# Cross attention of a decoder layer: outputs turned and divided in 32x32 blocks on VectorE instead of with TensorE transposes

## The chip, the cores and the metric

One core of a Trainium2 chip runs the whole program. The metric is device time in microseconds (us), and shares are of the profiled execution's span. Everything is float32.

## What is computed

The program is one layer of a decoder over 32 sequences of 128 tokens by 512 features: self attention, cross attention, and a mixture of experts. Each of the three adds its result to x. The change lies in cross attention, which reads each sequence as 128 channels by 512 positions:

```python
def _L0_xattn_ref(x, c, Wq, bq, Wk, bk, Wv, bv, Wo, bo):   # x, c: (32, 128, 512)
    ...
    q = split_heads(_proj(x, Wq, bq))      # 8 heads of 16 channels
    k = split_heads(_proj(c, Wk, bk))
    v = split_heads(_proj(c, Wv, bv))
    q = _apply_rotary(q_emb, q)
    k = _apply_rotary(k_emb, k)
    scores = jnp.einsum('bhtc,bhsc->bhts', q, k) / math.sqrt(K_CH)
    p_attn = jax.nn.softmax(scores, axis=-1)
    out = jnp.einsum('bhts,bhsc->bhtc', p_attn, v)
    out = out.transpose(0, 1, 3, 2).reshape(b, N_HEADS * K_CH, t_t)
    return _proj(out, Wo, bo)
...
x = x + _L0_xattn_ref(_layernorm(x), ctx_2048, ...)
```

## The kernel before, in words

**Stages.** Self attention runs first, then cross attention (from about 942 us to about 2145 us of the span), then the experts. Routing of the tokens to the experts (class Routing) is done in small steps inside the cross-attention stage.

**Cross attention.** For each sequence b, the eight heads are held as four pairs of 32 rows; one head of each pair is "side" 0, the other is side 1. A unit of work is a step (b, side, c, pair): 2 sides, 4 chunks c of 128 positions and 2 pairs of row groups make 16 steps for a sequence and 512 in all. In step n

- `maxima` multiplies q and k (L615, two matmuls of 32 rows x 128 columns by 512) and VectorE takes the negated row maxima straight from PSUM (L619, 128x1024);
- `exponentials` multiplies k and q again for the step 11 earlier (L638), and ScalarE takes exponentials from PSUM (L642, 128x1024).

The maxima of a side are turned with TensorE (`turn_maxima`, L83 on nm) and added into q (L627), so that the second product comes out with its maximum taken off. When all eight steps of a side are through, `weigh` multiplies the exponentials with the values (L653, 32 matmuls of 32 columns in two halves). The values carry a block of ones beside each head's 16 channels, so that of the 32 rows of a row group 16 are the head's outputs and the others its sum. The result is one PSUM tile of 128 rows by 512 positions per side, and still has to be divided by the sums.

**Division before the change.** ScalarE copies each side's result to SBUF (`xu`, L659). `divide` turns both sides with eight 128x128 TensorE transposes (L668) into one PSUM tile, so that positions lie on partitions and the sums in columns; VectorE takes their reciprocal (L671) and multiplies (L674, once for each side, from PSUM) into `xo`. `turn_out` turns `xo` back with four transposes (L83 on xo) and ScalarE copies that to `xoT` (L682). `leave` multiplies with the output weights (L691), and VectorE adds bias and residue (L695).

**What sets the order.** The order on TensorE, VectorE, ScalarE and GpSimd in this stage is the order of the calls (`tc.manual_schedule`). `plan` gives each piece of work of sequence b a step, counted from the sequence's own first step (16 b); `advance` then runs step n as: first half of `weigh` if one is due, the "sooner" calls, `maxima`, `exponentials`, second half of `weigh`, the "later" calls. Counted modulo 16, so that "step 13" is the step with remainder 13, the work falls as follows (each entry is for some earlier or later sequence):

| step | before maxima | maxima, exponentials | after |
|---|---|---|---|
| 13 | weigh side 1, first half; slots_of, measure_out, rotate q | yes | weigh side 1, second half, then copy to xu; groups |
| 14 | | yes | values |
| 15 | | yes | divide; normalize_out; enter |
| 0 | | yes | turn_out |
| 1 | | yes | turn_maxima side 1; enter |
| 2 | | yes | leave |
| 3, 4 | | yes | at 4: project k; enter |
| 5 | weigh side 0, first half; choose, rotate k, measure | yes | weigh side 0, second half, then copy to xu; take |
| 6 | | yes | hand_over (L83 on h); enter |
| 7, 8 | | yes | count (L934), then router (L718) |
| 9 to 12 | | yes | turn_maxima side 0, project q, enter |

Those VectorE operations of these calls that matter below: `groups` is five small ones (L878, L879, L881, L885, L887), `take` two (L922 with two SBUF inputs, L927).

**PSUM.** All tiles of PSUM come from one pool of four buffers of two banks each (`banks()`, L50). A new tile takes the buffer whose last reader stands earliest in the order of the calls. In the built program the matmuls of `exponentials` (L638) therefore wait in most steps for VectorE, and those of `maxima` (L615) in most steps for ScalarE.

Of the kernel before, what the change touches and what calls it, by code (L numbers as in the profile page):

```python
# [10 lines left out]
F32 = mybir.dt.float32  # L11
I32 = mybir.dt.int32
AF = mybir.ActivationFunctionType
ALU = mybir.AluOpType
# [4 lines left out]
P = 128  # L19
E = 512  # L20
# [82 lines left out]
def self_attention(cm, x, x1_d, Wq, Wk, Wv, Wo, lq1, lk1, lq2, lk2, heads, beside):  # L103
# [13 lines left out]
    with ExitStack() as ctx:  # L117
# [301 lines left out]
        for n in range(len(steps) + 5):  # L419
# [11 lines left out]
            if 2 in at:  # L431
                weigh(*at[2])
            if k % 2:
                values(g + 1, k // 2)
            elif 5 in at:
                leave(at[5][0])
            if 3 in at and at[3][1]:
                scale_out(at[3][0])
            if 2 in at:
                divide(*at[2])  # L440
                if at[2][1]:
                    finish(at[2][0])
            b = (g + 2) * G + k // 2
            if k % 2 == 0:
                measure(b)
                if 4 in at:
                    load_again(at[4][0])
            else:
                normalize(b)
                turn_in(b)  # L450
                load(b + G)
                if 4 in at:
                    turn_out(at[4][0])
# [4 lines left out]
class CrossAttention:  # L458
# [10 lines left out]

    NH, C = 8, 16
    TC = EC
    S = 2 * TC
    Q = P // 32
# [169 lines left out]
    def weigh(self, b, side, half):  # L645

        TC, Q, po = self.TC, self.Q, self.po
        if half == 0:
            po[b, side] = self.cm.banks()[:, 0, :]
        for c in (2 * half, 2 * half + 1):  # L650
            es = [self.expd.pop((b, side, c, pair)) for pair in range(2)]
            for j in range(Q):
                self.nc.tensor.matmul(  # L653
                    po[b, side][ts(j, 32), :], self.v2[b % 2][:, c, 2 * j + side, :],
                    es[j // 2][:, j % 2, :], start=c == 0, stop=c == TC - 1,
                )
        if half:
            self.out[b, side] = self.p2.tile([P, E], F32, name="xu")
            self.nc.scalar.copy(self.out[b, side], po.pop((b, side)))  # L659

    def divide(self, b):

        nc, TC, Q, C, out = self.nc, self.TC, self.Q, self.C, self.out
        tr = self.cm.banks()
        for side in range(2):
            u = out.pop((b, side))
            for c in range(TC):
                nc.tensor.transpose(tr[:, side, ts(c, P)], u[:, ts(c, P)], self.cm.ident)  # L668
        tr = tr.rearrange("p s (x r) -> p s x r", r=2 * C)
        rs = self.p2.tile([P, 2, TC * Q], F32, name="xrs")  # L670
        nc.vector.reciprocal(rs, tr[:, :, :, C])  # L671
        out[b] = self.p2.tile([P, TC * Q, 2, C], F32, name="xo")
        for side in range(2):
            nc.vector.tensor_tensor(  # L674
                out[b][:, :, side, :], tr[:, side, :, 0:C],
                rs[:, side].unsqueeze(2).broadcast_to([P, TC * Q, C]), ALU.mult,
            )

    def turn_out(self, b):
        tr = self.cm.turn4(self.out.pop(b).rearrange("p x s c -> p (x s c)"))  # L680
        self.out[b] = self.p2.tile([P, self.TC, P], F32, name="xoT")
        self.nc.scalar.copy(self.out[b], tr)  # L682

    def load_again(self, b):
        self.x1[b] = self.p2.tile([P, E], F32, name="x1")
# [2 lines left out]
    def leave(self, b):  # L688

        py = self.cm.banks()[:, 0, :]  # L690
        self.nc.tensor.matmul(  # L691
            py, self.wT["o"], self.out.pop(b).rearrange("p t x -> p (t x)"), start=True, stop=True
        )
        x1 = self.x1[b]
        self.nc.vector.scalar_tensor_tensor(x1, py, self.bo, x1, ALU.add, ALU.add)  # L695
        self.nc.sync.dma_start(out=self.x2_d[b], in_=x1)
# [471 lines left out]
class Experts:  # L1168
# [11 lines left out]
    Q = 4  # L1180
# [390 lines left out]
```

## Time and profile before

| | |
|---|---|
| runs of the kernel before | 4184.48 us median of 3 (4179.18 to 4187.29) |
| the profiled execution | 4186.66 us, span 4184.9 us, granted clock 0.991 |
| busy over the span: TensorE, VectorE, ScalarE, GpSimd | 4079.9, 2093.0, 1296.3, 2247.7 us |
| eight transposes in divide (L668), for one sequence | 1.02 us from the first to the next matmul's start |
| four transposes in turn_out (L83 on xo), for one sequence | 0.56 us likewise |
| ScalarE copies L659 and L682 | 585 ns and 581 ns |
| VectorE in divide: L671, L674 (twice) | 358 ns, 419 ns each |
| maxima on VectorE, L619 | 1225 ns |

A row of the timeline gives the start in us, how long it took, the engine and line, the operation, what it writes and reads, and, in brackets, how long the engine had been idle and what ended that. Rows that follow each other at once with the same operation are merged. A row of a group gives busy time, mean duration in ns and the idle time before it. A row of the waits gives who waited for whom: the sum, how often, and the longest. In this stage a TensorE row's own bracket shows little, since a product's rows overlap and the weight loads (PEld) do the waiting; the distance between the starts of rows is what measures TensorE's progress.

### The profile page before, as it was taken

To read this page: it belongs to the slowest core of one execution; us is meant where nothing else is said; L and a number is where in the kernel's file an instruction comes from. 1 tells how busy PE (TensorE), PEld (TensorE's weight loads), DVE (VectorE), ACT (ScalarE), POOL (GpSimd) and SP (SyncE) were. 2 spreads that over 40 slices of the span, in tenths; PEclk is the share of its full clock that TensorE was granted. 3 is DMA by queue.
4 is the path that set the end of the run, shared out by engine and by line. 5 is a ranking of instruction groups with operands and counts; after the bars stand their busy time and mean duration, and the time that the engine had idled before them with its cause. 6 is when DMAs were issued, how large, how long until landed. Compare 5 with 4: busy or idle time off the path is not lost. (4 is left out here: it accounts for less than half of the span.)

```text
span 4184.9 us, 60374 instructions
## 1 busy us (share of the span) xinstructions
PE 4079.9 (97%) x21044; PEld 2154.4 (51%) x21044; DVE 2093.0 (50%) x3394; ACT 1296.3 (31%) x1855; POOL 2247.7 (54%) x2388
## 2 busy tenths in 40 slices
PE   7999999989999999999989999999999999999999
PEld 5666666653343444443434555555555555554444
DVE  4556555567788888888841333333333333332111
ACT  2333333334565555555630111111111111111000
POOL 3444444343455555555542777777777777773000
PEclk9999999999999999999999999999999999999999
DMA  3000000012111111111114677776776776775110
GB/s 103 26 29 29 29 31 29 16 36 82 41 44 46 44 44 41 44 44 44 36 61 145 164 168 171 165 186 159 169 168 164 168 182 154 185 164 130 60 61 30
DMA packets 282791, 386.33 MB, mean 92 GB/s; under 512 B 147792, under 2 KB 175056, under 8 KB 282448
## 3 DMA queue, kind: packets, MB, share of 16 engines
q0 software_dynamic: 62912, 109.85, 14.6%
q1 hardware_dynamic: 77680, 186.52, 13.6%
q10 hardware_dynamic: 141888, 86.01, 7.4%
q8 instruction: 170, 2.79, 0.3%
q14 instruction: 141, 1.16, 0.1%
HBM read 616.47 MB, written 142.02 MB: 181 GB/s over the span
## 5 line engine op out<-in xcount | busy, mean ns | idle before, releaser
L1304 POOL DMA_INDIRECT e_xr<-h_d,e_run_of x832 | 849.5, 1021 | 296.3 <-issue 246.2
L619 DVE TENSOR_REDUCE nm<-ps 128x2 f32<-128x1024 f32 x512 | 623.7, 1225 | 200.0 <-PE ps L615 131.9
L642 ACT ACTIVATE xp<-ps 128x1024 f32<-128x1024 f32 x512 | 517.1, 1024 | 422.3 <-PE ps L638 421.9
L1334 DVE TENSOR_TENSOR e_gu<-e_act,ps 128x352 f32<-128x352 f32 x208 | 108.6, 522 | 947.8 <-ACT e_act L1333 947.8
L1365 PE MATMUL ps<-wd,e_guT 128*128 128x512 f32 (+1 forms) x1248 | 570.2, 592 | 2.4 <-issue 2.3
L615 PE MATMUL ps<-xk,xq 32*128 32x512 f32 x2048 | 561.4, 635 | 1.6 <-POOL x_ln_down L66 1.1
L638 PE MATMUL ps<-xqn,xk 32*128 32x512 f32 x2048 | 548.8, 639 | 0.6 <-DVE xqn L627 0.6
L1329 PE MATMUL ps<-wg,e_xT 128*128 128x352 f32 x1664 | 529.0, 460 | 4.0 <-DMA wg<-in_L_ffn_w_gate_dram 4.0
L1329 PE MATMUL ps<-wu,e_xT 128*128 128x352 f32 x1664 | 527.2, 460 | 1.6 <-DMA wu<-in_L_ffn_w_up_dram 1.6
L1329 PEld LDWEIGHTS ps<-wg,e_xT 128*128 128x128 f32 x1664 | 315.4, 190 | 239.0 <-issue 105.9
L1329 PEld LDWEIGHTS ps<-wu,e_xT 128*128 128x128 f32 x1664 | 316.1, 190 | 179.7 <-DMA wu<-in_L_ffn_w_up_dram 4.3
L1370 POOL DMA_INDIRECT sum_d<-e_y,e_into x208 | 338.4, 1627 | 118.0 <-issue 70.3
L1333 ACT ACTIVATE e_act<-ps 128x352 f32<-128x352 f32 x208 | 96.4, 463 | 902.6 <-PE ps L1329 797.2
L1365 PEld LDWEIGHTS ps<-wd,e_guT 128*128 128x128 f32 (+1 forms) x1248 | 237.0, 190 | 247.4 <-issue 205.4
L1369 ACT ACTIVATE e_y<-ps,e_weight 128x512 f32<-128x512 f32 x208 | 142.9, 687 | 411.7 <-PE ps L1365 398.0
L615 PEld LDWEIGHTS ps<-xk,xq 32*128 32x128 f32 x2048 | 157.9, 183 | 212.1 <-ACT xp L642 100.7
L951 POOL DMA_INDIRECT table_d<-entry,at x192 | 196.6, 1024 | 109.9 <-DMA table_d<-entry,at 55.7
L1355 DVE STREAM_TRANSPOSE e_guT<-e_gr 96x384 f32<-96x384 f32 (+1 forms) x416 | 230.5, 554 | 47.7 <-DMA e_gr<-e_gu_d 40.4
L653 PE MATMUL ps<-xp,v 128*32 128x512 f32 x2048 | 248.1, 601 | 1.6 <-ACT xp L642 1.2
L1316 DVE STREAM_TRANSPOSE e_xT<-e_xr 128x512 f32<-128x512 f32 x208 | 226.9, 1091 | 6.5 <-DMA e_xr<-h_d,e_run_of 6.5
L229 POOL TENSOR_SCALAR k<-kz,a_keep,a_extra 128x256 f32<-128x256 f32 x128 | 83.4, 660 | 252.3 <-ACT kz L228 246.3
L228 ACT ACTIVATE kz<-ps,a_keep 128x256 f32<-128x256 f32 x128 | 53.7, 470 | 410.9 <-PE ps L222 410.9
(267 smaller groups left out, 5316.8 us busy)
## 6 DMA issues: line engine op xcount, KB each, us to landing
wg<-in_L_ffn_w_gate_dram SPq DMA_DIRECT2D x208, 704.0 KB
wu<-in_L_ffn_w_up_dram SPq DMA_DIRECT2D x208, 704.0 KB
wd<-in_L_ffn_w_down_dram SPq DMA_DIRECT2D x208, 576.0 KB
e_gu_d<-e_gu ACTq DMA_DIRECT2D x208, 192.0 KB
e_gr<-e_gu_d ACTq DMA_DIRECT2D x208, 192.0 KB
wd<-in_L_ffn_w_down_dram SPq DMA_DIRECT2D x208, 128.0 KB
e_xr<-h_d,e_run_of POOLq DMA_INDIRECT x832
xin<-in_x_dram SPq DMA_DIRECT2D x32, 256.0 KB
```

What stands on the lines that cost most here:

```text
L615: self.nc.tensor.matmul(sc[:, i, :], q[rows, ts(c, P)], k[rows, :], start=True, stop=True)
L619: self.nc.vector.tensor_reduce(at[:, self.ROW[side], 2 * pair : 2 * pair + 2], sc, AX.X, ALU.max, negate=True)
L638: self.nc.tensor.matmul(sc[:, i, :], k[rows, ts(c, P)], q[rows, :], start=True, stop=True)
L642: self.nc.scalar.activation(e, sc, AF.Exp)
L653: self.nc.tensor.matmul(po[b, side][ts(j, 32), :], self.v2[b % 2][:, c, 2 * j + side, :], es[j // 2][:, j % 2, :], start=c == 0, stop=c == ...
L951: self.nc.gpsimd.indirect_dma_start(out=self.table_ds[k % 2][:, :], out_offset=bass.IndirectOffsetOnAxis(ap=self.at[b][:, k : k + 1], axis=0),
L1304: self.cm.nc.gpsimd.indirect_dma_start(out=xr[:, t, :], out_offset=None, in_=self.h3_d.rearrange("t (q f) -> (t q) f", q=self.Q), in_offse ...
L1316: self.cm.nc.vector.transpose(xT.rearrange("p c (t i) -> p c t i", t=self.Q), self.xr.pop(i).rearrange("p t (j c) -> p c t j", c=EC),)
L1329: nc.tensor.matmul(pgu[:, half, 0:M], t[:, c, :], w[:, c, :], start=c == 0, stop=c == EC - 1)
L1355: self.cm.nc.vector.transpose(t[rows, 0:n, :].rearrange("p c (t i) -> p c t i", t=self.Q), g[rows, :, 0 : 32 * n].rearrange("p t (j c) -> ...
L1365: nc.tensor.matmul(py, t[:n, c, :], self.wd[s][:n, c, :], start=c == 0, stop=c == len(M_CHUNKS) - 1)
L1370: nc.gpsimd.indirect_dma_start(out=self.sum_d[:, :], out_offset=bass.IndirectOffsetOnAxis(ap=self.into[:, i : i + 1], axis=0), in_=y[:, :] ...
```

## The change

```diff
@@ weigh @@
         if half:
-            self.out[b, side] = self.p2.tile([P, E], F32, name="xu")
-            self.nc.scalar.copy(self.out[b, side], po.pop((b, side)))
+            if side == 0:
+                self.out[b] = self.p2.tile([P, 2, E // 32, 32], F32, name="xu", bufs=1)
+            self.nc.vector.transpose(
+                self.out[b][:, side].rearrange("p k r -> p (k r)"), po.pop((b, side))
+            )

     def divide(self, b):
-        nc, TC, Q, C, out = self.nc, self.TC, self.Q, self.C, self.out
-        tr = self.cm.banks()
-        for side in range(2):
-            u = out.pop((b, side))
-            for c in range(TC):
-                nc.tensor.transpose(tr[:, side, ts(c, P)], u[:, ts(c, P)], self.cm.ident)
-        tr = tr.rearrange("p s (x r) -> p s x r", r=2 * C)
-        rs = self.p2.tile([P, 2, TC * Q], F32, name="xrs")
-        nc.vector.reciprocal(rs, tr[:, :, :, C])
-        out[b] = self.p2.tile([P, TC * Q, 2, C], F32, name="xo")
-        for side in range(2):
-            nc.vector.tensor_tensor(
-                out[b][:, :, side, :], tr[:, side, :, 0:C],
-                rs[:, side].unsqueeze(2).broadcast_to([P, TC * Q, C]), ALU.mult,
-            )
+        nc, C = self.nc, self.C
+        u, n = self.out.pop(b), E // 32
+        rs = self.p2.tile([P, 2, n], F32, name="xrs")
+        nc.vector.reciprocal(rs, u[:, :, :, C])
+        self.out[b] = self.p2.tile([P, n, 2, C], F32, name="xo")
+        nc.vector.tensor_tensor(
+            self.out[b].rearrange("p k s c -> p s k c"), u[:, :, :, 0:C],
+            rs.unsqueeze(3).broadcast_to([P, 2, n, C]), ALU.mult,
+        )

     def turn_out(self, b):
-        tr = self.cm.turn4(self.out.pop(b).rearrange("p x s c -> p (x s c)"))
-        self.out[b] = self.p2.tile([P, self.TC, P], F32, name="xoT")
-        self.nc.scalar.copy(self.out[b], tr)
+        o = self.out.pop(b)
+        self.out[b] = self.p2.tile([P, E], F32, name="xoT")
+        self.nc.vector.transpose(self.out[b], o.rearrange("p k s c -> p (k s c)"))

     def leave(self, b):
         self.nc.tensor.matmul(
-            py, self.wT["o"], self.out.pop(b).rearrange("p t x -> p (t x)"), start=True, stop=True
+            py, self.wT["o"], self.out.pop(b), start=True, stop=True
         )
```

A head's 16 outputs and its sum lie in one group of 32 rows, so a turn within blocks of 32x32 is enough to bring position onto partitions and the sum into a column; the same turn undoes it. Each side's PSUM result is turned by VectorE into SBUF (one 128x512 instruction, unit steps on both ends) where ScalarE copied it; `divide` now reads SBUF only and multiplies both sides in one instruction of 128x512; `turn_out` is one VectorE instruction from SBUF to SBUF. For a sequence that is twelve TensorE transposes and three ScalarE copies fewer, three 128x512 turns on VectorE more, and one multiplication of 128x512 with two SBUF inputs in place of two of 128x256 with one from PSUM. `divide` and `turn_out` take no PSUM tile any more. The calls keep their steps; in the order on VectorE the new turns stand after the maxima of steps 13 and 5, ahead of `groups` and `take`, and after the maxima of step 0.

## The prediction

> **What bounds the kernel now.** I read the page's busy line first, then busy time by stretches of 100 us inside cross attention (1000 to 2100 us), then the waits there, then the timeline of one sequence.
>
> ```profile
> PE 4079.9 (97%) x21044; PEld 2154.4 (51%) x21044; DVE 2093.0 (50%) x3394; ACT 1296.3 (31%) x1855; POOL 2247.7 (54%) x2388
> ```
>
> ```profile
> sum 1100.00, PE 1080.57 PEld 443.05 DVE 881.30 ACT 647.08 POOL 597.20; mean PE 98.23 PEld 40.28 DVE 80.12 ACT 58.83 POOL 54.29
> ```
>
> ```profile
> PEld ps L574 <- DVE nm L619: 60.3, 58, 1.2
> ...
> PEld ps L638 <- DVE nm L619: 25.0, 87, 0.5
> ```
>
> VectorE is at 50% over the span but at 80% in this stage, and TensorE's weight loads wait for it there. So TensorE's 98% isn't the whole bound. The division's reciprocal (L671) starts at 1451.32, 1488.46, 1525.61 and 1562.74 us: a sequence takes 37.14 us. Where TensorE loses time within it, the timeline shows (I count from the first half of weigh in step 13, 1404.76 us, and write that time as 0):
>
> ```profile
> 1410.71 1.23 DVE L619 TENSOR_REDUCE nm<-ps 128x2 f32<-128x1024 f32 x1 [0.23 <-PE ps L638]
> 1411.69 0.70 PE L615 MATMUL ps<-xk,xq 32*128 32x512 f32 x2
> 1411.99 0.70 PE L638 MATMUL ps<-xqn,xk 32*128 32x512 f32 x2
> ```
>
> L638 of step 15 starts 0.05 us after the maxima of step 14 end. The same holds in steps 0, 1 and 2 (L619 at 1412.87, 1415.25, 1417.20; L638 at 1414.15, 1416.53, 1418.49): always 1.28 us after L619's start. Both products of a step take 1.07 us when they start together, as in step 14; here each step costs 0.3 to 0.5 more. Step 7 shows the same at its largest:
>
> ```profile
> 1428.28 1.34 DVE L922 TENSOR_TENSOR hits<-number,picked 128x192 f32<-128x192 f32 x1
> 1429.66 0.49 DVE L927 TENSOR_REDUCE taken<-hits 128x32 f32<-128x192 f32 x1
> 1430.07 1.22 DVE L619 TENSOR_REDUCE nm<-ps 128x2 f32<-128x1024 f32 x1
> ```
>
> ```profile
> 1430.55 1.13 PE L615 MATMUL ps<-xk,xq 32*128 32x512 f32 x4
> 1431.35 1.13 PE L638 MATMUL ps<-xqn,xk 32*128 32x512 f32 x4
> ```
>
> L638 comes 0.8 us after L615, 1.28 after an L619 that `take` held up. The bound is the loop L619 -> L638 of the next step, with TensorE and VectorE taking turns as the late one.
>
> **What the Trainium skill says.** VectorE: DVE Perf Modes, "The three transpose paths", gives 311 ns for a VectorE turn of 128x128 in bf16, in 32x32 blocks only. At one element a cycle of 0.96 GHz, 384 more columns give an estimate of 311 + 400 = 711 ns for 128x512. The trace has STREAM_TRANSPOSE only with stepped inputs: 1091 ns for 128x512 (L1316, step of four elements). The same page's errata section times a float32 tensor_tensor as (N+151)/0.96 ns: 691 for 512; the trace agrees (L348, 688). SBUF — State Buffer, "Who interferes with whom", says that a VectorE instruction with two SBUF inputs contends with a GpSimd instruction that reads SBUF. The trace agrees: L922 takes 348 ns at least and 1340 at the median; here it ends 0.22 us after GpSimd's L586 (1428.13 to 1429.40).
>
> **The price of a turn (T).** Upper end: 1.09 us, L1316. But stepped reading explains that row: L927 reads 192 elements 32 apart in 491 ns, L945 reads 192 neighbours in 344; 147 ns over 192 is 0.77 ns an element, and 512 such would add 0.39 us. 1.09 less 0.39 is 0.70. STREAM_SHUFFLE of 128x512 with unit steps takes 0.73, PSUM sources are no slower (L627, 0.68). I take 0.70; lower end 0.65.
>
> **Part by part, for a sequence.** Removed from TensorE: 1.02 us (L668) and 0.56 us (turn_out), 1.58 in all. Removed from ScalarE: three copies of 0.58; at 59% busy with 391 us of waiting for L638 in the stage it sets nothing, so nothing. VectorE: three turns (2.10) and one multiplication of 0.69 come, two of 0.42 go, the reciprocal stays (L879, the same size from SBUF, takes 353 ns against 358): +1.95 us on 29.8. What counts is where these stand.
>
> *Steps 13 to 2.* Before: L619 of step 14 starts at 5.95, of step 1 at 12.44, L638 of step 2 at 13.73, leave at 14.78. After: the turn needs the end of weigh's second half, whose copy started at 4.91 (1409.67). VectorE, which was in `groups` from 4.17 on, stands until 4.91. The turn ends at 5.61. `groups`, 1.55 us before, 1.45 now (L878 was stretched to 0.47 by GpSimd's L585; now it waits for L586 until 5.93), ends at 7.06 instead of 5.72. L619 of step 14 starts at 7.10, 1.15 late; that of step 15 at 8.25. L638 of step 15 starts at 7.10 + 1.28 = 8.38 and its rows are needed by L615 of step 0, which starts 0.97 later (as L615 of step 4 after step 3), 9.35: before, with the eight transposes between, 9.31. So divide's gain is eaten here. VectorE: L619 of step 15 to 9.40, reciprocal 0.39, multiplication 0.63 (slot of 0.69), 10.42; L619 of step 0 at 9.35 + 1.17 = 10.52, to 11.67; the turn of turn_out to 12.37; L619 of step 1 at 12.37. That is 0.07 before the old 12.44. So 1.58 us of TensorE work buys 0.07 us: L638 of step 2 and leave follow by 1.28 and 1.05, and from leave on the timeline is the old one. With T = 1.09 both turns count, +0.78.
>
> *Steps 5 to 8.* Nothing leaves TensorE here. L619 of step 5 ends its slot at 23.53 as before; then VectorE stands until weigh's second half is through (copy at 1429.03: 24.27), and turns until 24.97. Only now comes L922. GpSimd is then in the first of two L592 (0.76 us each from 1429.52: 24.76 to 25.52), which read SBUF. I let L922 take its turn at 25.52 and end 0.22 later, at 25.74, against 24.86 before: +0.88. L619 of step 6, L638 of step 7 and count move with it, since L638 was the late one there already; steps 8 to 12 are spaced by TensorE and keep the shift. If no collision comes: 24.97 + 0.33 = 25.30, +0.44. If both L592 go first: 26.27 + 0.22, +1.63.
>
> *Sum.* `take` falls into 30 of these stretches (first at step 53, every 16 to step 517): 30 x 0.88 = 26.4. `groups` falls into 31: 31 x -0.07 = -2.2. The first sequence's stretch has no `groups`: 1.45 less on VectorE, some -0.9. The last division comes after the stage, beside matmuls alone: -1.6. Together +21.7 on 4186.66, 4208.4; the median of the runs lies 2.2 below the profiled execution: 4206.2, I say 4206 (+0.5%).
>
> **Rivals.**
> (a) *TensorE's saving comes through.* For it: 98% busy, VectorE idle for a fifth. If `groups` and the turns keep off the path in steps 13 to 2, TensorE's own sum holds there: -1.58 + 0.88 for step 5, -0.70 x 31 = -22, 4163; with step 5 hidden too, -1.58 x 32 = -51, 4134. Against: L619 -> L638 above. It decides at the start of L619 of step 1: every 0.1 us earlier than 12.4 is 3 us.
> (b) *L922 finds GpSimd free:* +0.44 in place of +0.88, 4206 - 13 = 4193, the edge of no change.
> (c) *Turns cost what L1316 costs:* three times 0.39 on the path, 1.17 x 31 = +36, 4242.
> (d) *L922 waits for both L592:* +0.75 x 30 = +22, 4229. The new multiplication has two SBUF inputs as well; at 9.8 it meets GpSimd's L951 (9.64 to 10.76). If that blocks it, up to 0.9 us more, 31 x 0.9 = +28, 4234.
>
> **How the numbers follow.** Forecast with errors of a tenth or two a sequence (4194 to 4220): 0.42. (c), (d) or both in part: 0.26. (b), 4176 to 4193: 0.15. (a): 0.17. A measurement of this kernel tells about 0.2% (8.4 us) from no change. So slower 0.68, same 0.15, faster 0.17. The range leaves out most of (a) and (c) with (d): 4170 to 4243. Slower cases hold most of the chance; their own range is 4194 to 4243.
>
> **What would show it.** Right: a sequence takes about 37.9 us; STREAM_TRANSPOSE of xu near 0.70; VectorE idle ahead of xu, released by L655 (the new number of L653); L922 starts after the turn and ends after a GpSimd L594; L640 of step 15 starts 1.28 after L621 of step 14, which follows L887 at once; ScalarE's copies gone and not missed. Wrong: the maxima of step 14 not later than before, a sequence under 37 us, or turns of 1 us.

## The result and the profile after

| | before | after |
|---|---|---|
| median of 12 runs each | 4187.39 us (4179.18 to 4192.06) | 4178.35 us (4175.28 to 4181.71) |
| the profiled execution | 4186.66 us, span 4184.9 | 4178.81 us, span 4177.1 |
| a sequence in the stage | 37.14 us | 37.06 us |

The ratio of the times is 0.9981, with an interval of 0.9972 to 0.9990: 0.2% faster, at the edge of what can be told from no change. The forecast was 4206 and slower; the time lies within the range of 4170 to 4243, but on the other side of the kernel before. Lines after the change are counted in its own listing: L621 takes the maxima (L619 before), L617 and L640 are the two products (L615 and L638), L655 weighs (L653), L662 and L682 are the new turns, L672 and L674 divide.

The busy line of the page, and below it the sum of busy times from 1000 to 2100 us:

```profile
PE 4063.7 (97%) x20660; PEld 2115.6 (51%) x20660; DVE 2113.8 (51%) x3458; ACT 1236.4 (30%) x1759; POOL 2253.9 (54%) x2388
```

```profile
sum 1100.00, PE 1075.97 PEld 411.84 DVE 902.11 ACT 593.75 POOL 605.45; mean PE 1075.97 PEld 411.84 DVE 902.11 ACT 593.75 POOL 605.45
```

Work has moved as the change says: in the stage VectorE has 20.8 us more to do (902.11 against 881.30) and ScalarE 53.3 less. TensorE lost twelve of its short rows in every sequence, and yet it is shown as busy for 1075.97 of 1100 us against 1080.57. Its saving went into waiting, as the waits of the same stretch show:

```profile
ACT xp L644 <- PE ps L640: 489.9, 356, 2.7
...
PEld ps L640 <- DVE nm L621: 77.3, 88, 1.0
```

The second product's weight loads waited 25.0 us for the maxima before and wait 77.3 now. ScalarE waits 99 us longer than before for the same product (489.9 against 390.8): the copies it was spared were not missed.

**Where the 7.85 us between the two profiled executions come from.** I compare the starts of `leave`'s product (L691) in both traces, sequence by sequence, with what the prediction's sum gives for the same stretch:

| stretch | predicted | measured |
|---|---|---|
| before the stage: start of the first maxima, 942.22 and 940.15 us | 0 | -2.07 |
| to the third `leave` (no `take` yet) | -0.9 - 2 x 0.07 = -1.0 | -1.41 |
| 27 sequences, to the 30th `leave` | 27 x (0.88 - 0.07) = +21.9 | -2.18 |
| the last two divisions and what follows | 3 x 0.88 - 2 x 0.07 - 1.6 = +0.9 | -1.68 - 2.40 + 1.89 = -2.19 |
| sum | +21.7 (rounded terms) | -7.85 |

The first row has nothing to do with the change, since no changed operation has run by then; the first maxima stand anywhere from 939.4 to 942.6 us in the traces of this study. (The medians of twelve differ by 9.04; the twelve of one kernel spread over 12.9 us before and 6.4 us after.) Most of the error, 24 of 29.6 us, lies in the third row: a sequence became 0.08 us shorter where 0.81 more was forecast.

**Steps 13 to 2 after the change.** The timeline of VectorE for one sequence. The first half of `weigh` in step 13 starts at 1400.98 us, which is time 0 below.

```profile
1405.89 0.72 DVE L662 STREAM_TRANSPOSE xu<-ps 128x512 f32<-128x512 f32 x1 [0.66 <-PE ps L655]
1406.53 0.45 DVE L878 TENSOR_SCALAR score<-score 128x32 f32<-128x32 f32 x1
...
1407.98 2.34 DVE L621 TENSOR_REDUCE nm<-ps 128x2 f32<-128x1024 f32 x2
1410.24 0.34 DVE L672 RECIPROCAL xrs<-xu 128x32 f32<-128x32 f32 x1
1410.62 0.75 DVE L674 TENSOR_TENSOR xo<-xu,xrs 128x512 f32<-128x512 f32 x1
1411.29 1.21 DVE L621 TENSOR_REDUCE nm<-ps 128x2 f32<-128x1024 f32 x1
1412.43 0.69 DVE L682 STREAM_TRANSPOSE xoT<-xo 128x512 f32<-128x512 f32 x1
1413.05 1.18 DVE L621 TENSOR_REDUCE nm<-ps 128x2 f32<-128x1024 f32 x1
```

From the turn on there is no bracket of idle time in these rows: VectorE works without a pause from 4.91 to 12.07 (the start of the maxima of step 1) and beyond. TensorE in the same stretch, the products of steps 15 and 2 and `leave`:

```profile
1409.24 1.36 PE L640 MATMUL ps<-xqn,xk 32*128 32x512 f32 x8 [0.20 <-DVE nm L621]
...
1414.29 1.13 PE L640 MATMUL ps<-xqn,xk 32*128 32x512 f32 x4
1415.34 1.12 PE L691 MATMUL ps<-xoT,oT 128*128 128x512 f32 x2
```

L640 of step 15 comes 1.26 us after the start of the maxima of step 14 (1407.98), and L640 of step 2 1.24 us after those of step 1 (1413.05). At these two places TensorE follows VectorE, as forecast. In between it is ahead: the product for the maxima of step 1 starts at 9.66 (the timeline merges its rows with those of step 0), and VectorE takes it up only at 12.07. There TensorE's saving went into waiting.

**Step 5 after the change.** VectorE, and GpSimd at the same time:

```profile
1424.83 0.72 DVE L662 STREAM_TRANSPOSE xu<-ps 128x512 f32<-128x512 f32 x1 [0.66 <-PE ps L655]
1425.47 0.32 DVE L922 TENSOR_TENSOR hits<-number,picked 128x192 f32<-128x192 f32 x1
1425.82 0.49 DVE L927 TENSOR_REDUCE taken<-hits 128x32 f32<-128x192 f32 x1
1426.24 2.51 DVE L621 TENSOR_REDUCE nm<-ps 128x2 f32<-128x1024 f32 x2
```

```profile
1423.93 1.27 POOL L588 TENSOR_TENSOR rot<-rot,rot 128x512 f32<-128x512 f32 x1
1425.31 1.70 POOL L594 TENSOR_SCALAR xk<-rot,keep,extra 128x512 f32<-128x512 f32 x2
```

GpSimd in step 5 before the change, when L922 ran from 1428.28 to 1429.62:

```profile
1428.13 1.27 POOL L586 TENSOR_TENSOR rot<-rot,rot 128x512 f32<-128x512 f32 x1
1429.52 1.51 POOL L592 TENSOR_SCALAR xk<-rot,keep,extra 128x512 f32<-128x512 f32 x2
```

Here is the term that failed. L922 takes 0.32 us with GpSimd's L594 running beside it. Before, it took 1.34 because it met GpSimd's TENSOR_TENSOR (L586 there, L588 here); the turn ahead of it has moved it past that, and the TENSOR_SCALAR that follows doesn't hold it up. The moment of meeting is nearly the same: L922 starts 0.15 us after L586 before and 0.16 us after L594 now. What differs is GpSimd's operation.

The durations of the two new turns and of L922, with least, median and greatest in ns:

```profile
L662 DVE STREAM_TRANSPOSE xu<-ps x64: 716/716/718, 987.2 to 2134.8; 128x512 f32<-128x512 f32 x64
...
L682 DVE STREAM_TRANSPOSE xoT<-xo x32: 694/695/712, 1008.9 to 2136.7; 128x512 f32<-128x512 f32 x32
...
L922 DVE TENSOR_TENSOR hits<-number,picked x32: 314/316/360, 1091.9 to 2176.2; 128x192 f32<-128x192 f32 x32
```

### The profile page after: what moved, and what is told of

Its sections match the earlier page's. It is cut to its first block, busy times and chain, and to the rows that moved or that the text cites. A ratio compares the mean times of both kernels' runs of the same rounds, so it can differ in the third digit from the quotient of the medians.

```text
span 4177.1 us, 59576 instructions
## 1 busy us (share of the span) xinstructions
PE 4063.7 (97%) x20660; PEld 2115.6 (51%) x20660; DVE 2113.8 (51%) x3458; ACT 1236.4 (30%) x1759; POOL 2253.9 (54%) x2388
## 5 line engine op out<-in xcount | busy, mean ns | idle before, releaser
L621 DVE TENSOR_REDUCE nm<-ps 128x2 f32<-128x1024 f32 x512 | 617.8, 1218 | 116.8 <-PE ps L617 63.0
L617 PE MATMUL ps<-xk,xq 32*128 32x512 f32 x2048 | 534.2, 630 | 1.9 <-POOL x_ln_down L66 1.0
L640 PE MATMUL ps<-xqn,xk 32*128 32x512 f32 x2048 | 521.8, 637 | 9.5 <-DVE nm L621 6.6
L617 PEld LDWEIGHTS ps<-xk,xq 32*128 32x128 f32 x2048 | 159.7, 183 | 211.2 <-ACT xp L644 105.3
L655 PE MATMUL ps<-xp,v 128*32 128x512 f32 x2048 | 247.1, 598 | 3.3 <-ACT xp L644 2.9
L951 POOL DMA_INDIRECT table_d<-entry,at x192 | 198.5, 1034 | 79.8 <-issue 55.7
L640 PEld LDWEIGHTS ps<-xqn,xk 32*128 32x128 f32 x2048 | 150.8, 183 | 121.0 <-DVE nm L621 79.7
```

Source lines behind the costliest of these rows:

```text
L617: self.nc.tensor.matmul(sc[:, i, :], q[rows, ts(c, P)], k[rows, :], start=True, stop=True)
L621: self.nc.vector.tensor_reduce(at[:, self.ROW[side], 2 * pair : 2 * pair + 2], sc, AX.X, ALU.max, negate=True)
L640: self.nc.tensor.matmul(sc[:, i, :], k[rows, ts(c, P)], q[rows, :], start=True, stop=True)
L655: self.nc.tensor.matmul(po[b, side][ts(j, 32), :], self.v2[b % 2][:, c, 2 * j + side, :], es[j // 2][:, j % 2, :], start=c == 0, stop=c == ...
```

## The experiments

Three accounts of why a sequence became 0.08 us shorter stand in the expectations. V: VectorE's order of rows sets steps 13 to 2, TensorE's freed time is worth next to nothing there, and L922 no longer waits. T: TensorE's own work sets the pace, so its freed 1.58 us count, and VectorE has time to spare. W, formed after the first four runs: both engines' work lies on one chain that changes from one to the other, so that both count nearly in full.

I measure by the **period**, the median distance between the starts of `leave`'s product in a profile. It repeats within 0.01 to 0.02 us (37.06 in both traces of the kernel after), and one term of it is worth about 31 times its size in the total. The runs come from different chips: the kernel before took 4184.42 us beside the first four runs, 4239.0 beside the next four and 4235.71 beside the last four. So only ratios, each to the kernel before on the same chip, and periods are compared.

### Is the turn in step 0 on the path? (e1_turn_twice)

```diff
+        for _ in range(2):
             self.nc.vector.transpose(self.out[b], o.rearrange("p k s c -> p (k s c)"))
```

> turn_out's turn is done twice into the same tile, one more VectorE turn of 0.69 us in step 0 of every sequence, nothing else. Theory V (VectorE's order from step 13 to step 2 holds TensorE back): L621 of step 1 comes 0.6 to 0.7 later in 30 sequences, about +20 us on 4178. Rival T (TensorE's own work sets the pace, VectorE has a fifth of its time free): nothing, within 4 us of 4178.

Period 37.80, 0.75 more than after; 4205.14 us, ratio 1.0057 (1.0044 to 1.0071). VectorE and TensorE in step 0 and after:

```profile
1423.68 1.44 DVE L683 STREAM_TRANSPOSE xoT<-xo 128x512 f32<-128x512 f32 x2
1425.05 1.19 DVE L621 TENSOR_REDUCE nm<-ps 128x2 f32<-128x1024 f32 x1
```

```profile
1426.29 1.13 PE L640 MATMUL ps<-xqn,xk 32*128 32x512 f32 x4 [0.71 <-DVE nm L621]
```

The second turn moves the maxima of step 1, and TensorE stands 0.71 us for them. A turn at this place counts in full, as V says. 31 x 0.75 = 23 us explain 0.55 of the 0.76% by which its ratio lies above that of after. Three single sequences of 39.2 to 39.3 us are part of the rest (see the end).

### Was it L922 that failed to wait? (e3_take_first)

Side 0's turn is called after `take`, so that L922 stands where it stood before the change:

```diff
+            if not (side == 0):
+                self.turn_side(b, side)
...
+            later.put(at + 5, self.turn_side, b, 0)
```

> Side 0's turn is called after take, so that L922 stands ahead of it in step 5 as it did before the change. Theory V: L922 meets GpSimd's third product of rotate again and takes 1.3 us instead of 0.32, the turn comes after it, L621 of step 6 starts 0.2 to 0.3 later in 29 sequences: +7 us, about 4185. Rival (L922 is short because of something other than where it stands): it stays at 0.32 and L621 of step 6 comes up to 0.4 earlier, -11 us, about 4167.

Period 37.29, 0.23 more than after; 4188.03 us, ratio 1.0007 (0.9999 to 1.0015). In this listing `take` is L927 and L932, and the turn is L666:

```profile
1466.32 1.34 DVE L927 TENSOR_TENSOR hits<-number,picked 128x192 f32<-128x192 f32 x1
1467.69 0.50 DVE L932 TENSOR_REDUCE taken<-hits 128x32 f32<-128x192 f32 x1
1468.10 0.71 DVE L666 STREAM_TRANSPOSE xu<-ps 128x512 f32<-128x512 f32 x1
```

```profile
1466.17 1.27 POOL L588 TENSOR_TENSOR rot<-rot,rot 128x512 f32<-128x512 f32 x1
1467.55 1.51 POOL L594 TENSOR_SCALAR xk<-rot,keep,extra 128x512 f32<-128x512 f32 x2
```

The wait is back: 1.34 us, to 1467.66, which is 0.22 after L588 ends. Here L594 takes 1.51 for its pair where it took 1.70 with L922 beside it. So the turn's place ahead of `take` turned a wait of about one microsecond into a useful 0.64. The total grew with the period: 0.23 x 29 = 7 us of the 11 between the two ratios.

### Do the groups behind the turn in step 13 cost anything? (e4_groups_first)

```diff
+            if not (side == 1):
+                self.turn_side(b, side)
...
+            later.put(at + 13, self.turn_side, b, 1)
```

The call stands after `groups` of the same step.

> Side 1's turn is called after groups, so that groups fills the time in which VectorE stands waiting for the end of weigh in step 13. Theory V: L621 of step 14 starts 0.6 to 0.7 earlier, leave with it, in 30 sequences: about -18 us, 4160. Rival T: nothing, within 4 us of 4178.

Period 37.06: no gain, where V expected some 0.6. VectorE from the turn (L666) on, and TensorE's product for the maxima of step 15:

```profile
1445.49 0.70 DVE L666 STREAM_TRANSPOSE xu<-ps 128x512 f32<-128x512 f32 x1
1446.12 1.19 DVE L621 TENSOR_REDUCE nm<-ps 128x2 f32<-128x1024 f32 x1
1447.94 1.23 DVE L621 TENSOR_REDUCE nm<-ps 128x2 f32<-128x1024 f32 x1 [0.64 <-PE ps L617]
```

```profile
1446.77 1.13 PE L617 MATMUL ps<-xk,xq 32*128 32x512 f32 x4
```

The maxima of step 14 do come 0.7 us earlier (at 6.29, not 7.00). Those of step 15 stay at 8.11, because their product only starts at 6.94, behind `values`, and is ready 1.17 later. In the kernel before they stood at 8.11 too (1412.87 us). So the chain passes from TensorE to VectorE at this product, and what VectorE does before 8.11 is free up to there: the turn of side 1 costs nothing in the kernel after. V missed this.

The time, 4183.04 us, ratio 0.9999 (0.9991 to 1.0007), is longer than the period gives; its runs spread from 4177.34 to 4190.83. No run of after stood beside it on that chip, so this difference in the total stays open, and I use the period alone.

### What is TensorE's freed time worth? (e7_tensor_turns_back)

The twelve transposes are put back on TensorE, beside the new turns, and nobody reads them:

```diff
     def divide(self, b):
+        tr = self.cm.banks()
+        for side in range(2):
+            flat = u[:, side].rearrange("p k r -> p (k r)")
+            for c in range(self.TC):
+                self.nc.tensor.transpose(tr[:, side, ts(c, P)], flat[:, ts(c, P)], self.cm.ident)
...
     def turn_out(self, b):
+        self.cm.turn4(o.rearrange("p k s c -> p (k s c)"))
```

> The twelve TensorE transposes of a sequence are put back at their old places as extra work with a result that nobody reads (and with the PSUM tiles they took); VectorE's turns stay. Theory V: TensorE was waiting there anyway, so they cost little: +0.1 to 0.4 us a sequence, 4181 to 4191. Rival T: the saving was worth what TensorE lost, so they cost up to 1.58 us a sequence, +30 to +50, above 4208.

Period 38.28, 1.22 more than after; 4213.11 us, ratio 1.0072 (1.0058 to 1.0085). That is far from V's "next to nothing" and below T's 1.58. TensorE, then VectorE, from the second product of step 15 on (time 0 is 1414.68):

```profile
1422.95 1.13 PE L640 MATMUL ps<-xqn,xk 32*128 32x512 f32 x4 [0.20 <-DVE nm L621]
1424.01 1.09 PE L675 MATMUL ps<-ident,xu 128*128 128x128 f32 x8
1425.03 0.70 PE L617 MATMUL ps<-xk,xq 32*128 32x512 f32 x2
```

```profile
1426.21 1.23 DVE L621 TENSOR_REDUCE nm<-ps 128x2 f32<-128x1024 f32 x1 [1.13 <-PE ps L640]
```

The eight transposes (L675) push the product of step 0 (L617) to 1425.03, and VectorE stands 1.13 us for it. (The bracket names L640, which ran beside that product.) TensorE's rows follow one another without a gap here, so it is TensorE's time that is missing, not a PSUM tile, though this run takes those again too. The maxima of step 0 start at 11.53 instead of 10.31: nearly all of the 1.22 us is lost in this one place. The four of `turn_out` cost nothing visible; `leave` is late by the same 1.22. So V's claim on TensorE's worth falls, and its claim on the turn in step 0 stands.

### A turn where VectorE is idle (e2_turn_idle)

One useless turn, of a table in SBUF, in step 11, where VectorE stands 0.99 us:

```diff
+    def idle_turn(self, b):
+        spare = self.p2.tile([P, E], F32, name="xoT")
+        self.nc.vector.transpose(spare, self.cos["k"])
...
+            later.put(at + 11, self.idle_turn, b)
```

> The same extra turn of 0.69 us as in the run that turned twice, but called in step 11, where VectorE stands 1.0 us a sequence before the maxima of step 12. Theory W (a VectorE operation counts in full where the maxima of the next step wait for VectorE, steps 15 to 1, and for nothing where they wait for TensorE): the period of a sequence stays at 37.06 us, 4178 to 4183. Rival (VectorE is simply full): +0.7 us a sequence, as in step 0, about 4200.

Period 37.05; 4231.63 us, ratio 0.9985 (0.9977 to 0.9993), which is that of after. A fourth turn at this place is free. W was right.

### No turn on either engine (e8_no_turns)

This leaves the turning out altogether: both sides are copied by ScalarE, and `turn_out` only renames. What is divided and handed on is then not the layer's, the routing differs, and with it the experts' stage; only the period of this stage is read.

```diff
-            self.nc.vector.transpose(
+            self.nc.scalar.copy(
...
-        o = self.out.pop(b)
-        self.out[b] = self.p2.tile([P, E], F32, name="xoT")
-        self.nc.vector.transpose(self.out[b], o.rearrange("p k s c -> p (k s c)"))
+        self.out[b] = self.out.pop(b).rearrange("p k s c -> p (k s c)")
```

> All turns are left out, those of TensorE and those of VectorE: ScalarE copies each side to SBUF as before the change, divide works on the unturned copy, and turn_out does nothing, so the output is not the layer's. Theory W: the saving on TensorE and the cost of the turns on VectorE both count nearly in full, so without either a sequence takes 1.0 to 1.3 us less than 37.06, about 4140 to 4148. Rival T (the turns on VectorE are hidden, and TensorE's 1.58 us were hidden before as well): 37.0 us, 4176 to 4182.

Period 36.12 (the whole took 4412.73 us, ratio 1.0415, 1.0391 to 1.0438, for the reason given). W had expected 1.0 to 1.3 less than after; it is 0.94. The rival, for which everything was hidden, is out. With this the four cases are complete:

| period, us | no turns on VectorE | turns on VectorE |
|---|---|---|
| turns on TensorE | 37.14 (before) | 38.28 (e7) |
| none on TensorE | 36.12 (e8) | 37.06 (after) |

TensorE's turns are worth 1.02 or 1.22 of the 1.58 us that they take. VectorE's cost 0.94 or 1.14 of the 2.1 that they take. The change exchanges one for the other. That is where its gain went. The four corners differ in a little more than the turns (before divides from PSUM in two multiplications and has ScalarE copy three results, e8 has it copy two), which may be why each difference comes out in two sizes.

The trace of e8 also shows which turns cost something. The maxima of step 0 start at 10.32 with no turn at all and at 10.31 in after: side 1's turn costs nothing. The second product of step 2 starts at 12.71 instead of 13.31: `turn_out` costs 0.60. From `project k` on, steps 5 to 12 take 18.84 us in before and e8, 19.18 in after and e7: side 0's turn costs 0.34, and TensorE's transposes do not touch this stretch.

### Division later (v2_divide_later)

Division, `turn_out` and `leave` go from steps 15, 0 and 2 to steps 8, 9 and 10 of the next round, where VectorE has idle time; `xu` gets two buffers, `xo` and `xoT` one each.

```diff
-            later.put(at + 15, self.divide, b)
-            later.put(at + 16, self.turn_out, b)
-            later.put(at + 18, self.leave, b)
+            later.put(at + 24, self.divide, b)
+            later.put(at + 25, self.turn_out, b)
+            later.put(at + 26, self.leave, b)
```

> divide, turn_out and leave are called in steps 8, 9 and 10 of the following sequence in place of 15, 0 and 2 (xu gets two buffers, xo and xoT one). Theory W: the reciprocal, the multiplication, the turn and the residue (2.4 us of VectorE) leave the chain from the maxima of step 15 to the product of step 2 and go where VectorE stands idle for up to 0.8 us a step: 1.0 to 1.5 us less a sequence, period about 35.8, 4135 to 4150. Rival (a step is bound by the way from its maxima's product to the next step's exponentials' product, 2.45 us, whatever stands on VectorE): period 36.8 to 37.1, 4168 to 4180.

Period 36.76, 0.30 less than after; 4226.53 us, ratio 0.9968 (0.9955 to 0.9981). W missed with 35.8; its rival, 36.8 to 37.1, came closer. From step 13 to `project k` a sequence takes 16.18 us instead of 17.88, a gain of 1.70, and the rest takes 20.58 instead of 19.18, a loss of 1.40. In both, 1.06 are `leave`'s own product, which only changed its place. What remains is a gain of 0.64 and a loss of 0.34. VectorE in steps 0 and 1 (time 0 is 1398.21):

```profile
1408.62 2.36 DVE L621 TENSOR_REDUCE nm<-ps 128x2 f32<-128x1024 f32 x2 [0.96 <-PE ps L617]
```

The gain is small because TensorE is the late one at once. Reciprocal and multiplication are gone from between the maxima of steps 15 and 0, and those of step 0 still start at 10.41 (10.31 in after): they now stand 0.96 us for their product. Only the turn of step 0 is saved. In steps 9 and 10 VectorE has no idle time left, and the maxima of step 10 start 1.63 us after their product, where it is 1.17 in after; this fits the loss of 0.34, though no run separates it.

### Side 0 turned where VectorE is idle (v3_side0_idle, v3_again)

ScalarE copies side 0 out of PSUM again, and VectorE turns the copy from SBUF in step 11:

```diff
             if side == 0:
+                self.flat[b] = self.p2.tile([P, E], F32, name="xf", bufs=1)
+                self.nc.scalar.copy(self.flat[b], po.pop((b, 0)))
...
+            later.put(at + 11, self.turn_first, b)
```

> Side 0 is copied to SBUF by ScalarE as before the change, and VectorE turns it from SBUF in step 11; side 1 is left as in the changed kernel. Theory W: the turn of side 0 costs 0.35 us a sequence in steps 5 to 8 and nothing in step 11; L922 goes back to 1.34 us, which the maxima of step 6 can bear (before the change they waited for TensorE at the same moment): period about 36.7, 4167 to 4172. Rival (L922's wait takes the place of the turn): period 37.0 to 37.3, 4177 to 4186.

> Side 0 by ScalarE and turned in step 11, again, beside the changed kernel: a sequence 36.70 us, 0.36 us less in 29 sequences, about 0.9955 of the kernel before.

Periods 36.70 and 36.72, 0.36 and 0.34 less than after (steps 5 to 12 take 18.84 us again); ratios 0.9956 (0.9944 to 0.9969) and 0.9953 (0.9941 to 0.9966), 4221.68 and 4216.52 us on two chips. W was right. VectorE in steps 5 to 11 of the second of these runs (L932 is `take`'s first, L671 the turn of side 0):

```profile
1423.01 1.33 DVE L932 TENSOR_TENSOR hits<-number,picked 128x192 f32<-128x192 f32 x1
...
1426.45 1.23 DVE L621 TENSOR_REDUCE nm<-ps 128x2 f32<-128x1024 f32 x1 [0.43 <-PE ps L617]
...
1435.42 0.70 DVE L671 STREAM_TRANSPOSE xu<-xf 128x512 f32<-128x512 f32 x1
1436.48 1.23 DVE L621 TENSOR_REDUCE nm<-ps 128x2 f32<-128x1024 f32 x1 [0.35 <-PE ps L617]
```

`take` pays its wait for GpSimd again (1.33 us), and that is borne: the second maxima after it still wait 0.43 us for TensorE. The turn stands in what was idle time, of which 0.35 us is left.

### Both, and `leave` a round later (v6_both_idle, v7_next_round, c_after_again)

v6 puts v2 and v3 together, with one buffer of `xu`. v7 is v6 with `leave` 16 steps after its old place and everything behind it moved by 16 too. c_after_again is the kernel after, unchanged.

```diff
+            later.put(at + 11, self.turn_first, b)
+            later.put(at + 24, self.divide, b)
+            later.put(at + 25, self.turn_out, b)
+            later.put(at + 26, self.leave, b)
```

In v7 the last of these lines is `later.put(at + 34, self.leave, b)`.

> The changed kernel again, beside the two that follow: 0.998 of the kernel before, a sequence 37.06 us.

> Side 0 turned in step 11, and divide, turn_out and leave in steps 8, 9 and 10 of the following sequence. Of the run with the three alone the stretch from step 13 to project k is 1.70 us shorter and the rest 1.39 longer, most of it the 1.06 us of leave's product and what VectorE has more there. Theory W: side 0's turn is apart from that, the gains add: 36.4 us. Rival (VectorE is the late one in steps 8 to 11 by then, and the turn makes it worse): 36.7 to 37.0.

> As the run before, but leave stays in step 2, sixteen steps later than before, and all that follows it moves by sixteen steps too. Theory W: TensorE waits in steps 1 to 4 anyway, so leave's product is cheaper there than in step 10: 35.8 to 36.2 us a sequence; one more sequence is finished behind the stage, some 5 to 10 us once: 0.990 to 0.994 of the kernel before. Rival (the product of leave costs its 1.06 us wherever it stands): as the run before.

| | period | median, us | ratio to before |
|---|---|---|---|
| c_after_again | 37.06 | 4228.47 | 0.9983 (0.9977 to 0.9990) |
| v3_again | 36.72 | 4216.52 | 0.9953 (0.9941 to 0.9966) |
| v6_both_idle | 36.40 | 4206.89 | 0.9934 (0.9922 to 0.9946) |
| v7_next_round | 36.55 | 4216.07 | 0.9954 (0.9941 to 0.9967) |

The kernel after gives the ratio of the first measurement again, on another chip. The gains of v2 and v3 add up: 0.30 + 0.36 = 0.66, and v6 has 37.06 - 36.40 = 0.66. v6 beats both kernels. VectorE in v6, first in the steps of its old backlog, then in the division (L681 multiplies, L689 turns):

```profile
1440.60 2.36 DVE L621 TENSOR_REDUCE nm<-ps 128x2 f32<-128x1024 f32 x2 [0.96 <-PE ps L617]
...
1459.08 0.69 DVE L681 TENSOR_TENSOR xo<-xu,xrs 128x512 f32<-128x512 f32 x1
1459.69 1.22 DVE L621 TENSOR_REDUCE nm<-ps 128x2 f32<-128x1024 f32 x1
1460.82 0.70 DVE L689 STREAM_TRANSPOSE xoT<-xo 128x512 f32<-128x512 f32 x1
```

Where VectorE worked without a pause in after it now stands 0.96 us for TensorE (the first row); the division and its turn lie in steps 8 and 9.

v7 missed: 36.55 where 35.8 to 36.2 was expected, and it is slower than v6. `leave`'s product costs its time wherever it stands: back in step 2 it makes the stretch from step 13 to `project k` 1.25 us longer than in v6 and the rest 1.11 shorter. Of the 9.2 us between the medians the period explains some 4; that the sequence more that is left to be finished behind the stage makes the rest is not shown.

## Why the prediction was wrong

**The step that failed: "I let L922 take its turn at 25.52 and end 0.22 later, at 25.74 ...: +0.88".** L922 waited for nothing. Counted from `project k` in both kernels, the stretch through steps 5 to 12 grew by 0.34 (from 18.84 to 19.18 us), not by 0.88. Rival (b), "L922 finds GpSimd free: +0.44", had the right size for a reason that was not mine: GpSimd wasn't free, its L594 ran and didn't disturb. The same holds for (d): the new multiplication took 756 ns at the median and 769 at most beside GpSimd's L951, so nothing of a blocked 0.9 us came. My ground was a sentence in the Trainium skill, SBUF — State Buffer, "Who interferes with whom": a VectorE instruction with two SBUF inputs contends with a GpSimd instruction that reads SBUF. The sentence does not say that VectorE is the one that waits; I read that into it. In these runs VectorE waits beside GpSimd's TENSOR_TENSOR (1340 ns before, 1338 in e3), and not beside its TENSOR_SCALAR (316 ns), where GpSimd takes longer instead (1.70 us for its pair, not 1.51). This is 0.54 of the 0.89 us by which a sequence was mis-sized, 27 x 0.54 = 15 us.

The trace of before could have told. At the border of self attention and this stage another VectorE operation with two SBUF inputs (L374) meets first L592 itself, then a TENSOR_TENSOR:

```profile
909.66 1.28 POOL L592 TENSOR_SCALAR xk<-rot,keep,extra 128x512 f32<-128x512 f32 x1
909.69 0.69 DVE L374 SCALAR_TENSOR_TENSOR an<-at,rr 128x512 f32<-128x512 f32 x1 [5.09 <-POOL rr L368]
```

```profile
953.98 1.26 POOL L577 TENSOR_TENSOR rot<-rot,cos 128x512 f32<-128x512 f32 x1
954.04 1.74 DVE L374 SCALAR_TENSOR_TENSOR an<-at,rr 128x512 f32<-128x512 f32 x1 [3.02 <-POOL rr L368]
```

Beside L592 it takes its 0.69 us, as in 29 other cases beside a TENSOR_SCALAR, and L592 takes 1.28 instead of 0.76; beside L577 it takes 1.74. The prediction looked at L922 alone.

**A term mis-sized: steps 13 to 2, -0.07 forecast, -0.42 measured.** The order of the chain was right, with each time within 0.34 us of its place:

| start, from the first half of weigh | before | forecast | after |
|---|---|---|---|
| turn of side 1 | - | 4.91 | 4.91 |
| maxima of step 14 | 5.95 | 7.10 | 7.00 |
| maxima of step 15 | 8.11 | 8.25 | 8.11 |
| maxima of step 0 | 10.49 | 10.52 | 10.31 |
| maxima of step 1 | 12.44 | 12.37 | 12.07 |
| second product of step 2 | 13.73 | 13.65 | 13.31 |
| leave | 14.78 | 14.70 | 14.36 |

The 0.34 by which `leave` beats the forecast gather in small amounts. The next row starts 0.08 us before a turn's duration is over (1412.43 to 1413.05: 0.62 for a turn of 0.695), so two turns cost 0.06 and 0.08 less than the 0.70 that I used; for the multiplication I had used the slot, for the turns I had not. The two maxima in a row and the start of the first one give 0.08. The wait of 0.10 for the product of step 0 didn't come, since its product was 0.12 earlier than I had it. The last product followed by 1.24, not 1.28. Against that, reciprocal and multiplication took 1.05 instead of 1.02. This is 0.35 of the 0.89, 27 x 0.35 = 9 us. Neither term alone turned the sign: with the first put right the sum for a sequence would still have been +0.27, with the second +0.46.

**Rival (a), TensorE's saving comes through.** In its own form, -1.58 with the turns hidden, it didn't happen. Its point of decision was "every 0.1 us earlier than 12.4 is 3 us": the maxima of step 1 came 0.37 earlier, and the -0.42 at `project k` that follows from it is just enough to outweigh the +0.34 of step 5. In my own working the 1.58 us of TensorE work "buys 0.07". e7 shows what is true and false in that: put back, they cost 1.22. The saving is real, and the turns spend it. The forecast counted only the net of the two, and so couldn't see that a turn moved to an idle place (v3) would keep part of the saving.

**What was right.** None of the signs named for being wrong came (the maxima of step 14 are later, a sequence is not under 37 us, the turns are not 1 us): they could not tell a sequence of 37.06 from the 37.9 that was forecast. The price of a turn: 0.70 taken, 0.716 and 0.695 measured. Rival (c), 1.09, is out. The Trainium skill, VectorE: DVE Perf Modes, "The three transpose paths", had given an estimate of 711 ns by way of its bf16 figure; the trace agrees. ScalarE's copies were not missed. VectorE's idle stretch of 0.66 us ahead of the turn, released by the weighing, is there, and L640 of step 15 follows 1.26 after the maxima of step 14 (1.28 forecast). A counting slip: `take` first comes at step 69, not 53, which makes 29 instances, not 30. At the edges the first three sequences gave -1.41 against -1.0, and the end -2.19 against +0.9.

**The cause as the runs leave it.** TensorE and VectorE work one chain in turns: product of the maxima, L621, second product of the next step, the product after that. What stands on this chain counts in full while its engine is the late one, and for nothing beyond the point where the other becomes late (v2, e4). So twelve transposes off TensorE gain about 1.0 to 1.2 us (in e7 all of it by the eight of `divide`), the turns on VectorE cost about as much (side 1: 0, by e4 and e8; `turn_out`: 0.60 by e8, and 0.75 for a second one in e1; side 0: 0.34, by v3), and the sum is 0.08. Not tried: smaller or more PSUM tiles, which might loosen the chain itself.

## What to carry to other kernels

When work moves from one engine to another on a chain that both share, price both sides by their place on the chain and not by the busy shares: TensorE at 98% gave back two thirds of what was taken from it, and VectorE at 80% charged in full for one turn, half for another and nothing for the third. The gain then has to be collected by putting the new work into the receiving engine's idle steps, which here gained three times as much again as the change itself (ratio 0.9934 against 0.9983). How much of this `divide` and `leave` would have gained in the kernel before, with TensorE's transposes, was not tried. A wait seen between two engines holds for the pair of operations that showed it: look up which operation is on the other engine at the new time, and look in the same trace for another row that meets that operation, before carrying it over.

## What the runs showed of the hardware beyond this

- A VectorE tensor_tensor with two SBUF inputs (128x192) takes 1.34 us when it meets GpSimd's TENSOR_TENSOR of 128x512, and 0.32 when it meets GpSimd's TENSOR_SCALAR of the same size. In the second case GpSimd pays: its pair takes 1.70 us instead of 1.51. One of 128x512 (L374 before) shows the same: 1.74 us and 0.69.
- A float32 turn in 32x32 blocks of 128x512 takes 716 ns from PSUM and 695 from SBUF with unit steps, against 1091 in the experts' stage, where it reads with a step of four.
- In some runs single sequences took longer: 2.8 us in e3 and e4, about 1.4 in e1. In e4's trace TensorE's rows take about twice their time for some 7 us; a pair of these usually takes 0.70 or 0.59:

```profile
1379.87 1.22 PE L617 MATMUL ps<-xk,xq 32*128 32x512 f32 x2
1379.88 1.23 PE L640 MATMUL ps<-xqn,xk 32*128 32x512 f32 x2
```

The mean granted clock of the whole execution hides it (0.990 against 0.991 in after), but the clock of the stretch shows it: it is 0.50 from 1376.7 to 1383.5 us, and 1.00 from 1370 to 1376 and from 1384 to 1390. Between 1000 and 2080 us e4 has three such stretches of 6.83 us and e3 two; e1 has four of 3.41 us. The other traces have none there. So each long one costs 2.8 us and each short one about 1.4. Why the clock was halved at these moments stays open. It makes totals scatter by some microseconds, which is why the periods carry the argument.
